# A two-part sequence model on one core: the feed-forward's tile of 43 channels projected, activated and multiplied first, and the first chunk normalised 128 tokens at a time

## The chip, the core and the metric

The kernel runs on one core of a Trainium2 chip. The core has a matrix engine (TensorE; PE in the profile, and PEld for the loading of its weights), a vector engine (VectorE, DVE), a scalar engine (ScalarE, ACT), a general engine (GpSimd, POOL) and an engine that issues transfers (SyncE, SP). Each works through its own queue of instructions in order, and semaphores order them against each other. Matrix products land in PSUM, eight banks of 128 partitions by 512 floats; all else lies in SBUF. The metric is the device time of one execution in microseconds (us), the median of several runs; lower is better.

## What is computed

The input is two sequences of 4096 tokens with 256 channels, in float32. A recurrence layer (layer norm, three projections of the token mixed with the one before it, a scan in time, a group norm, an output projection) is followed by two layers of local attention with a feed-forward network. Cut to what bears on the change:

```python
x = x + _L0_attn_ref(_layernorm(x), ...)        # the recurrence, once per sequence
h = _layernorm(x)
for l in range(2):
    h = h + local_attention(shift_token(h) @ wqkv[l], ...) @ wo[l]   # windows of 128 tokens
    n = layernorm(shift_token(h)) * ln_g[l] + ln_b[l]
    a, g = jnp.split(n @ w1[l] + b1[l], 2, axis=-1)                  # 682 channels each
    h = h + (a * gelu(g)) @ w2[l] + b2[l]
x = x + h
```

The 682 channels of the feed-forward are five full tiles of 128 partitions and a rest. With a row of ones that carries the last bias, the rest has 43 rows; without it 42.

## The kernel before

**A plan first, then the program.** The kernel does not issue its instructions as it goes. It notes every operation with its engine, its operands and an estimated cost (`note` L238, `cost` L302), and a list scheduler (`order` L376) then chooses, engine by engine, the operation that can start first and, among equals, the one with the smaller place (`o.at`: a row number given by `plan.at`, then the order of noting). Operations marked `either` go to ScalarE or VectorE, whichever is free first in the plan. `give` (L514) issues the lot from one line, so almost every instruction of the profile carries L530, and groups are told apart by the tiles that they write and read. Because the whole program comes out of one plan, moving a few operations can change the order of others far away on every engine.

**The recurrence.** `Recurrence` (L597) handles a sequence in chunks: the first sequence in 512 tokens (256 for the last two chunks), the second in 256. `normed` (L640) is its layer norm. It takes two windows of 128 tokens at a time: for each window `bn_stats` and `bn_aggr` on VectorE into one half of `r_mv`, then for both at once the power of minus one half on GpSimd (`rsqrt_of`, L556: an addition, then the power, into `r_rs`), one small product on VectorE (`r_nb`), and one scaled copy on ScalarE for each window. `transposed` (L660) turns the normalised chunk on TensorE, and `project` (L707) multiplies it with the weights `wnow` and `wold`, which are first scaled by the mixing vectors (L1429 to L1432; `scaled`, an `either` operation).

**Attention and feed-forward.** The loop over `n` (L1480) takes 128 windows of 128 tokens: two sequences, two layers, 32 windows each. Four windows make a block of 512 tokens, `k`; there are 32 blocks. The feed-forward of a block runs one to two blocks behind its attention, spread as filler between the steps of later windows (`fill`, L1352):

- `gate` (L1281) projects one tile of 128 gate channels, 512 tokens wide, into `hm`.
- `remainders` (L1289) projects the 42 gate channels and the 42 value channels of the rest together (106 rows, with a gap) and copies them apart into `ends` and `rem`. There, even windows lie on partitions 0 to 42 and odd windows on 64 to 106, so each step on the rest takes two instructions of 42 rows.
- `gelus` (L1300) is one piece on ScalarE, never interrupted by other work: five activations on `hm`, then two on `ends`.
- `value` (L1310) projects one tile of value channels and multiplies it, with its bias, into `hm` on VectorE; for the last tile (`m` = 5) it multiplies `rem` into `ends`, with no projection of its own.
- `down_ends` (L1327) starts the output sums of two windows with the 64-row product of `ends` and `w2`; `down` (L1339) adds the five products with `hm`, adds the sum to `x` and stores it.

The last block has no later windows to hide in. `last_block` (L1376) takes it in two halves of 256 tokens: transposes of the normed input `h`, five gates, the remainders, the gelus, six values in order, the two `down_ends`, the two `down`. Its value products may be issued ahead of their gelus (`plan.early`, L1312).

Of the kernel before, what the change touches and what calls it, by code (L numbers as in the profile page):

```python
# [10 lines left out]
AF = mybir.ActivationFunctionType  # L11
ALU = mybir.AluOpType
# [3 lines left out]
P = 128  # L16
# [5 lines left out]
NM = 6  # L22
# [8 lines left out]
LN_EPS = 1e-5  # L31
# [25 lines left out]


SEM = 60
OWN = {"gpsimd": 75}  # L60
LEAN = 700
SLACK = 1.06
# [118 lines left out]
class Plan:  # L181
# [35 lines left out]
    def bank(self, shape):  # L217

        return self.view(Place(T, True), 0, shape)
# [10 lines left out]
    @contextmanager  # L230
    def piece(self):

        self.open = []
        yield
        self.open = None
# [140 lines left out]
    def order(self):  # L376
# [18 lines left out]
        def ready(g):  # L395
            for e in ("scalar", "vector") if g[0].eng == "either" else (g[0].eng,):
                t, off = 0.0, 0.0
                for o in g:
                    for d in o.deps:
                        if d.eng != e:  # L400
                            t = max(t, d.end + SEM - off)
                        elif e != "tensor" and owner[d] is not g:
                            t = max(t, d.end + OWN.get(e, 30))
                    off += o.step
                waiting[e].append((t, g))

        def earliest(e, t, g):
# [4 lines left out]
            if need:  # L412
                have = sorted(b for b in banks if b is not None)
                if len(have) < need:
                    return None
                t = max(t, have[need - 1] + SEM)
            return t
# [8 lines left out]
        while todo:  # L426
# [28 lines left out]
            e = min((e for e in engines if pick[e]), key=lambda e: pick[e][0], default=None)  # L455
            assert e is not None, "no operation can start"
            t, g = pick[e]
            for o in g:
# [11 lines left out]
                step, time = o.step, o.time  # L470
                if o.eng == "either" and e == "vector":
                    n = o.outs[0].idx.size
                    time = 150 + 1.04 * n if o.name == "copy" else 155 + 0.98 * n
                    step = time - 85
# [3 lines left out]
                if e not in ("tensor", "sync"):  # L478
                    step, time = step * SLACK, time * SLACK
# [10 lines left out]
                for p in o.uses:  # L490
                    c, last = counts[p]
# [42 lines left out]
def kernel(ctx: ExitStack, tc: tile.TileContext, a: dict, out: bass.AP):  # L534
# [6 lines left out]
    tile_of, bank, piece = plan.tile, plan.bank, plan.piece  # L541
# [14 lines left out]
    def rsqrt_of(dst, var, n, eps, op):  # L556

        nc.gpsimd.tensor_scalar(dst, var, eps, None, op)
        nc.gpsimd.tensor_tensor(dst, dst, mhalf[:, :n], ALU.pow)
# [37 lines left out]
    class Recurrence:  # L597
# [42 lines left out]
        def normed(self, c):  # L640
            nw = self.len[c] // P
            x = self.chunks[c]["x"]
            for w0 in range(0, nw, 2):
                ws = range(w0, min(w0 + 2, nw))
                mv = tile_of([P, 2, 2], "r_mv", 4)
                for w in ws:
                    st = tile_of([P, 6], "r_st", 4)
                    nc.vector.bn_stats(st, x[:, w, :])
                    nc.vector.bn_aggr(mv[:, w - w0, :], st)
                rs = tile_of([P, 2], "r_rs", 4)  # L650
                rsqrt_of(rs, mv[:, :, 1], 2, LN_EPS, ALU.add)
                nb = tile_of([P, 2], "r_nb", 4)
                nc.vector.scalar_tensor_tensor(nb, mv[:, :, 0], -1.0, rs, ALU.mult, ALU.mult)
                for w in ws:
                    i = w - w0
                    nc.scalar.activation(
                        x[:, w, :], x[:, w, :], AF.Identity, bias=nb[:, i : i + 1], scale=rs[:, i : i + 1]
                    )
# [190 lines left out]
    b1 = tile_of([P, L, 2, NM], "b1")  # L849
# [34 lines left out]
    ends = tile_of([P, NW // 2, P], "ends")  # L884
# [368 lines left out]
    def transpose_h(k, w0=0, w1=NW):  # L1253
        l = blocks[k][0]
        h = hs[k]
        if w0 == 0:
            hTs[k] = tile_of([P, 2, T], "hT")
        hT = hTs[k][:, :, w0 * P : w1 * P]
        for i in range(2):
            pt = bank([P, (w1 - w0) * P])  # L1260
            for w in range(w0, w1):
                nc.tensor.transpose(
                    pt[:, (w - w0) * P : (w - w0 + 1) * P], h[:, w, i * P : (i + 1) * P], ident
                )
            g, bb = lnp[:, l, 0, i : i + 1], lnp[:, l, 1, i : i + 1]
            if i == 0:
                nc.scalar.activation(hT[:, i, :], pt, AF.Identity, bias=bb, scale=g)
            else:
                nc.vector.tensor_scalar(hT[:, i, :], pt, g, bb, ALU.mult, ALU.add)

    def hidden(k, c0, cols, ts):
        pm = bank([P, ts.stop - ts.start])
        for i in range(2):
            nc.tensor.matmul(
                pm[:cols], w1[:, i, c0 : c0 + cols], hTs[k][:, i, ts], start=(i == 0), stop=(i == 1)
            )
        return pm
# [3 lines left out]
    def gate(k, m, ts=ALL):  # L1281
        either(hm[:, m, ts], hidden(k, m * P, P, ts))

    def halves(ts):

        pairs = slice(ts.start // (2 * P), ts.stop // (2 * P))
        return [(odd, slice(64 * odd, 64 * odd + HR), pairs) for odd in range(2)]

    def remainders(k, ts=ALL):  # L1289
        pm = hidden(k, G_LAST * P, HS, ts)  # L1290
        if ts.start == 0:
            rems[k] = tile_of([P, NW // 2, P], "rem")
        for odd, rows, pairs in halves(ts):
            nc.scalar.copy(ends[rows, pairs], of_half(pm[64:HS], odd))
            either(rems[k][rows, pairs], of_half(pm[:HR], odd))

    def of_half(t, odd):
        return t.rearrange("p (w two t) -> p w two t", two=2, t=P)[:, :, odd, :]

    def gelus(k, ts=ALL):  # L1300
        l = blocks[k][0]
        with piece():
            for m in range(NM - 1):
                g = hm[:, m, ts]
                nc.scalar.activation(g, g, AF.Gelu, bias=b1[:, l, 1, m : m + 1])
            for odd, rows, pairs in halves(ts):
                g = ends[rows, pairs]
                nc.scalar.activation(g, g, AF.Gelu, bias=b1[rows, l, 1, NM - 1 : NM])

    def value(k, m, ts=ALL):  # L1310
        l = blocks[k][0]
# [15 lines left out]
    def down_ends(n):  # L1327

        k, i = (n - NW) // NW - 1, n % NW
        if not 0 <= k < NK or i > 1:  # L1330
            return
        for odd in range(2):
            rows = slice(64 * odd, 64 * odd + 64)
            pys[k, 2 * i + odd] = bank([P, D])
            nc.tensor.matmul(
                pys[k, 2 * i + odd], ends[rows, i, :], w2[rows, NM - 1, :], start=True, stop=False
            )
# [38 lines left out]
    def last_block():  # L1376

        k = NK - 1
        for w in (0, 2):
            plan.at(NN + w)  # L1380
            ts = slice(w * P, (w + 2) * P)
            transpose_h(k, w, w + 2)
            for m in range(NM - 1):
                gate(k, m, ts)
            remainders(k, ts)
            gelus(k, ts)
            for m in range(NM):
                value(k, m, ts)
            down_ends(NN + NW + w // 2)
            down(k, w)  # L1390
            down(k, w + 1)
# [88 lines left out]
    for n in range(NN + 2):  # L1480
        k, w = divmod(n, NW)
# [16 lines left out]
        first, l = ahead and (n + 1) % (NB * NW) == 0, ((n + 1) // (NB * NW)) % L  # L1498
# [140 lines left out]
```

## Time and profile before

| what | value |
|---|---|
| runs | 2951.6, 2952.49, 3802.63 us; median 2952.49 us |
| the profiled execution | 2951.72 us; its span, first to last instruction, 2949.9 us |
| mean granted TensorE clock | 0.999 |
| VectorE busy | 2236.2 us, 76% |
| ScalarE busy | 2009.6 us, 68%; 112 loads of an activation table, 1.283 us each |
| GpSimd busy | 1496.6 us, 51% |
| mean busy share of the DMA engines | 2 tenths, 66 GB/s |
| one gelu on `hm`, 128x512 | 0.709 us (155 of them) |
| one gelu on `ends`, 42x256 | 0.498 us (62 of them) |
| a power on GpSimd, 128x2 in `r_rs` | 0.773 us (32 of them) |
| a power on GpSimd, 128x1 in `rs` | 0.615 us (192 of them) |

A time in the profile counts from the start of the span. In a timeline each row has the start, the time from the first start to the last end, the engine, the line, the operation, what it writes and reads, its shape, how many equal instructions follow each other (x), and in square brackets how long the engine sat idle before it and what ended that.

### The profile page before, as it was taken

How to read it: one execution, taken by the hardware profiler on the slowest of the kernel's cores; microseconds unless marked ns; L12 is line 12 of the kernel's file. 1: busy time of each engine (PE TensorE's matmuls, PEld its weight loads, DVE VectorE, ACT ScalarE, POOL GpSimd, SP SyncE). 2: the span in 40 equal slices, each digit the busy share in tenths (PEclk: the TensorE clock that was granted, in tenths of full speed). 3: DMA queues.
4: the chain of work that ended last, by engine and by line, in shares of the span. 5: the costliest groups of instructions: out<-in, count | busy, mean ns of one | idle time of the engine just before them, and what ended most of it. 6: DMA issues, size and time to landing. Idle time of an engine off the chain costs nothing.

```text
span 2949.9 us, 49361 instructions
## 1 busy us (share of the span) xinstructions
PE 2926.3 (99%) x15468; PEld 1908.8 (65%) x15468; DVE 2236.2 (76%) x5193; ACT 2009.6 (68%) x5281; POOL 1496.6 (51%) x1831
## 2 busy tenths in 40 slices
PE   9999999999999999999999999999999999999999
PEld 4476766666666666666666666666666666666666
DVE  7889999888866987786777767777776767676764
ACT  7877788778666877776566666665666666666664
POOL 2226755555554655555655444555554555555541
PEclk9999999999999999999999999999999999999999
DMA  2323332222221211111122221121112221111110
GB/s 82 112 76 121 114 96 75 85 68 64 65 64 55 76 53 51 59 58 57 55 77 79 76 68 48 59 61 58 58 47 66 63 64 53 58 54 52 53 41 24
DMA packets 191182, 195.13 MB, mean 66 GB/s; under 512 B 34756, under 2 KB 154436, under 8 KB 190408
## 3 DMA queue, kind: packets, MB, share of 16 engines
q1 hardware_dynamic: 190920, 191.98, 21.1%
q8 instruction: 123, 2.02, 0.3%
q14 instruction: 139, 1.14, 0.1%
HBM read 85.46 MB, written 39.85 MB: 42 GB/s over the span
## 4 chain that ended last, share of the span: by engine, by line
PE 86%; ACT 6%; DVE 5%; issue 1%; POOL 0%; DMA 0%; SPq 0%; ACTq 0%; DVEq 0%
PE bank L530 86%; ACT pr L530 1%; ACT pr L526 1%; ACT L530 1%; ACT hm L530 1%; DVE hm L530 1%; DVE arena L530 1%; DVE qk L530 1%; DVE bank L530 1%; DVE sq L530 0%; ACT arena L530 0%; ACT ends L530 0%; DVE h L530 0%; DVE pB L530 0%; DVE nmx L530 0%
## 5 line engine op out<-in xcount | busy, mean ns | idle before, releaser
L530 PE MATMUL bank<-wqkv,xT 128*128 128x512 f32 x1536 | 719.2, 595 | 0.5 <-ACT xT L530 0.5
L530 PE MATMUL bank<-hT,w 128*128 128x512 f32 (+3 forms) x1452 | 650.5, 580 | 0.0
L530 POOL TENSOR_TENSOR t<-qk,tab 128x256 f32<-128x256 f32 x512 | 390.5, 781 | 412.4 <-ACT qk L530 305.3
L530 ACT ACTIVATE pr<-bank,nmx 128x129 f32<-128x129 f32 (+1 forms) x1024 | 370.5, 379 | 136.5 <-DVE nmx L530 133.2
L530 PEld LDWEIGHTS bank<-hT,w 128*128 128x128 f32 (+1 forms) x1452 | 263.9, 188 | 246.7 <-issue 235.0
L530 PEld LDWEIGHTS bank<-wqkv,xT 128*128 128x128 f32 x1536 | 267.5, 191 | 212.7 <-issue 209.3
L530 POOL TENSOR_TENSOR rn<-rn,mhalf 128x16 f32<-128x16 f32 x128 | 395.1, 3087 | 9.0
L526 ACT ACTIVATE pr<-pr,sums 128x129 f32<-128x129 f32 (+1 forms) x957 | 334.2, 420 | 30.4 <-DVE pr L530 27.1
L530 DVE COPY_PREDICATED bank<-packs,bank 128x254 f32<-128x254 int32 x496 | 186.4, 420 | 214.1 <-PE bank L530 213.7
L530 PE MATMUL bank<-w,hm 128*128 128x256 f32 x1280 | 293.8, 380 | 0.0
L530 ACT COPY qk<-bank 128x512 f32<-128x512 f32 x224 | 131.7, 588 | 194.9 <-PE bank L530 172.5
L530 PEld LDWEIGHTS bank<-w,hm 128*128 128x128 f32 x1280 | 239.6, 190 | 33.2 <-issue 2.5
L530 POOL TENSOR_TENSOR dv<-vr,vt 128x512 f32<-128x512 f32 x124 | 163.7, 1320 | 187.8 <-PE bank L530 156.5
L530 DVE TENSOR_TENSOR pB<-bank,backs 128x512 f32<-128x512 f32 x248 | 170.1, 686 | 103.7 <-PE bank L530 73.1
L530 PE MATMUL bank<-kT,qT 64*128 64x256 f32 (+1 forms) x2048 | 246.1, 380 | 1.6 <-ACT qT L530 1.6
L530 PE MATMUL bank<-wo,oT 128*128 128x256 f32 x1024 | 242.6, 380 | 0.8 <-ACT oT L530 0.8
L530 PEld LDWEIGHTS bank<-wo,oT 128*128 128x128 f32 x1024 | 193.7, 190 | 67.0 <-issue 23.1
L530 PEld LDWEIGHTS bank<-kT,qT 64*128 64x128 f32 x2048 | 190.4, 187 | 70.8 <-issue 36.1
L530 ACT COPY hm<-bank 128x512 f32<-128x512 f32 (+1 forms) x180 | 103.8, 577 | 183.5 <-PE bank L530 181.7
L530 ACT ACTIVATION_READ_ACCUMULATOR pr<-bank,nmx 128x1 f32 x1024 | 221.0, 216 | 0.0
L530 ACT COPY pT<-bank 128x512 f32<-128x512 f32 x195 | 115.6, 593 | 130.8 <-PE bank L530 94.3
L530 PE MATMUL bank<-pT,vt 128*64 128x128 f32 x2048 | 203.3, 279 | 0.0
(160 smaller groups left out, 5635.2 us busy)
## 6 DMA issues: line engine op xcount, KB each, us to landing
vr<-vt SPq DMA_DIRECT2D x124, 224.0 KB
tab<-in_c_rot_dram SPq DMA_DIRECT2D x128, 128.0 KB
kT<-kT SPq DMA_DIRECT2D x64, 256.0 KB
z<-zd SPq DMA_DIRECT2D x16, 512.0 KB
x<-in_x_dram SPq DMA_DIRECT2D x16, 512.0 KB
x1d<-x SPq DMA_DIRECT2D x16, 512.0 KB
x<-x1d SPq DMA_DIRECT2D x16, 512.0 KB
h<-x SPq DMA_DIRECT2D x128, 64.0 KB
```

What stands on the lines that cost most here:

```text
L526: self.nc.scalar.activation(dst, src, AF.Copy, scale=scale)
L530: getattr(getattr(self.nc, o.eng), name)(*args, **kw)
```

## The change

```diff
@@ the planner
+CARE = 0
-                            t = max(t, d.end + SEM - off)
+                            t = max(t, d.end + SEM + (CARE if e == "tensor" else 0) - off)
@@ Recurrence.normed
-            for w0 in range(0, nw, 2):
-                ws = range(w0, min(w0 + 2, nw))
-                mv = tile_of([P, 2, 2], "r_mv", 4)
+            step = 1 if c == 0 else 2
+            for w0 in range(0, nw, step):
+                ws = range(w0, w0 + step)
+                mv = tile_of([P, 2, 2], "r_mv", 4)[:, :step]
                 for w in ws:
                     st = tile_of([P, 6], "r_st", 4)
                     nc.vector.bn_stats(st, x[:, w, :])
                     nc.vector.bn_aggr(mv[:, w - w0, :], st)
                 rs = tile_of([P, 2], "r_rs", 4)
-                rsqrt_of(rs, mv[:, :, 1], 2, LN_EPS, ALU.add)
-                nb = tile_of([P, 2], "r_nb", 4)
+                rs = rs[:, :step]
+                rsqrt_of(rs, mv[:, :, 1], step, LN_EPS, ALU.add)
+                nb = tile_of([P, 2], "r_nb", 4)[:, :step]
@@ gelus
         with piece():
+            for odd, rows, pairs in halves(ts):
+                g = ends[rows, pairs]
+                nc.scalar.activation(g, g, AF.Gelu, bias=b1[rows, l, 1, NM - 1 : NM])
             for m in range(NM - 1):
                 g = hm[:, m, ts]
                 nc.scalar.activation(g, g, AF.Gelu, bias=b1[:, l, 1, m : m + 1])
-            for odd, rows, pairs in halves(ts):
-                g = ends[rows, pairs]
-                nc.scalar.activation(g, g, AF.Gelu, bias=b1[rows, l, 1, NM - 1 : NM])
@@ last_block
             transpose_h(k, w, w + 2)
+            remainders(k, ts)
             for m in range(NM - 1):
                 gate(k, m, ts)
-            remainders(k, ts)
             gelus(k, ts)
-            for m in range(NM):
+            for m in (NM - 1, *range(NM - 1)):
                 value(k, m, ts)
```

`CARE` is zero and alters nothing. The first chunk of each sequence (`c == 0`: four windows in the first sequence, two in the second) is normalised one window at a time. `gelus` takes the rest before the full tiles in all 32 blocks. `last_block` also projects the rest before the gates and multiplies it before the full tiles; the fillers of the other 31 blocks (`fill`) keep their order of noting.

## The prediction, made before the change was run

> **What bounds the kernel now.** I read first the busy times of the page, then the busy times by stretch of the span, since an average hides stages, then the timelines of the first 16 us and the last 30 us, and one odd spot between.
>
> ```profile
> PE 2926.3 (99%) x15468; PEld 1908.8 (65%) x15468; DVE 2236.2 (76%) x5193; ACT 2009.6 (68%) x5281; POOL 1496.6 (51%) x1831
> ```
>
> ```profile
> 0.00:20.00 20.00, 13.43 (x28) 6.18 (x29) 9.53 (x30) 9.11 (x19) 4.70 (x23) 1.00 0.47 145
> 20.00:463.00 443.00, 436.26 (x1934) 277.58 (x1933) 396.44 (x865) 353.33 (x765) 200.20 (x288) 1.00 0.29 96
> 463.00:690.00 227.00, 225.86 (x1245) 148.28 (x1244) 201.09 (x465) 175.89 (x451) 130.45 (x164) 1.00 0.25 76
> 690.00:1864.00 1174.00, 1172.58 (x6364) 769.21 (x6362) 889.86 (x2090) 797.29 (x2155) 618.81 (x737) 1.00 0.21 63
> 1864.00:2468.00 604.00, 603.93 (x3301) 393.39 (x3302) 422.63 (x997) 384.45 (x1073) 318.01 (x369) 1.00 0.20 60
> 2468.00:2900.00 432.00, 429.83 (x2378) 277.41 (x2376) 303.65 (x717) 275.27 (x785) 221.43 (x247) 1.00 0.16 48
> 2900.00:2920.00 20.00, 20.00 (x118) 16.82 (x117) 4.81 (x13) 2.93 (x8) 3.00 (x6) 1.00 0.09 28
> 2920.00:2949.90 29.90, 24.43 (x112) 19.90 (x110) 8.22 (x21) 11.37 (x29) 0.00 (x0) 0.99 0.07 22
> ```
>
> In the second view a row holds the stretch, its length, then busy us and instructions of PE, PEld, DVE, ACT and POOL. Length less PE's busy time is PE's idle time: 6.6, 6.7, 1.1, 1.4, 0.1, 2.2, 0 and 5.5 us, together 23.6 of 2949.9. A busy PE need not be a fast one, so I checked the rows of the middle: in steady state a 128x512 product follows the last after 0.43 us, a 128x256 one after 0.215, without gaps, and those intervals times the counts fill the stretches. TensorE therefore bounds everything but both ends and a few small holes. The change takes no product away, so it can win only part of those 23.6 us, and loses whatever new idle time it opens on TensorE.
>
> **The tail.** This is the first half of the last block, where TensorE's queue has nothing else left.
>
> ```profile
> 2921.37 1.28 ACT L530 ACT_TABLE_LOAD   x1
> 2922.67 2.11 ACT L530 ACTIVATE hm<-hm,b 128x256 f32<-128x256 f32 x5
> ...
> 2924.68 0.81 ACT L530 ACTIVATE ends<-ends,b 42x128 f32<-42x128 f32 x2
> ...
> 2925.52 0.71 DVE L530 SCALAR_TENSOR_TENSOR ends<-rem,b,ends 42x128 f32<-42x128 f32 x2
> 2925.90 0.68 PEld L530 LDWEIGHTS bank<-w,ends 64*128 64x128 f32 x4 [2.46 <-DVE ends L530]
> 2925.91 1.08 PE L530 MATMUL bank<-w,ends 64*128 64x256 f32 x4 [2.23 <-DVE ends L530]
> ...
> 2926.91 4.58 PE L530 MATMUL bank<-w,hm 128*128 128x256 f32 x20
> ```
>
> ScalarE does the five gelus of `hm`, then the two of `ends`; VectorE multiplies `ends` last; the product that opens the output sums needs exactly that, and TensorE sits 2.23 us idle for it.
>
> In the changed program the rest is projected first. Its four copies (0.26 each) then lie among the gates' copies, which wait for products 0.86 apart anyway; the last gate copy ends near 2920.6 (the sixth product, as the sixth result before, whose first copy started at 2920.26, plus 0.37), so the table load starts 0.7 earlier. Gelus of `ends`: 2921.95 to 2922.75. Gelus of `hm`: 2922.75 to 2924.85, as late as before (2924.78). VectorE multiplies `ends` at about 2922.4 and 2922.8. The new order on TensorE is: five products of the window before (now 2920.92 to 2923.1, and kept), first `ends` product, two transposes of `h`, second `ends` product, two transposes, then `hm`. From the rows now, the four `ends` instructions with the way to `hm` take 1.0 us (2925.91 to 2926.91), the four transposes 0.45, and a second change between 64-row and full products half of that 1.0, 0.5: `hm` starts at 2923.1 + 1.95 = 2925.0, not 2926.91. Does it then wait for VectorE? The first `hm` multiplication needs gelu one (about 2923.2), fine; the fifth ends at about 2925.65, and the fifth product of the sum comes 4 x 2 x 0.215 = 1.7 us after the first, at 2926.7: covered by 1 us. Banks: five values, one old sum and one `ends` sum are held, so the second `ends` sum and the last transposes take banks that the first `hm` multiplication (2923.7) and the add to `x` (2924.0) free; both come in time. Gain 1.9 us.
>
> In the second half the `ends` load waited 0.23 for VectorE at 2941.44; that goes: 0.2 us. After it come, as now, 4.58 us of products, the last add of 0.42 and the last store. Tail: -2.1 us; bounds 0.3 (only the wait beyond the fifth `hm` multiplication goes) and 2.5 (both waits whole).
>
> **The gelus of the other 31 blocks.** Two gelus of `ends` now stand ahead of `hm`, so each gelu of `hm` comes 1.03 us later (two in one row take 1.03). What hides it: the first value multiplication starts 1.59 to 3.5 us after its gelu is done in every one of the 31 blocks; it waits for its projection. One example: gelus from 2072.41, the first done 2073.12, its multiplication at 2075.67. So at least 0.56 us of cover stays: cost 0. Without cover it would be up to 31 x 1.03 = 32 us, since the value products hold PSUM banks until they are multiplied.
>
> **The first layer norm.** Now:
>
> ```profile
> 4.49 0.72 POOL L530 TENSOR_TENSOR r_rs<-r_rs,mhalf 128x2 f32<-128x2 f32 x1
> ...
> 9.26 2.07 PE L530 MATMUL bank<-arena 128*128 128x512 f32 x2
> 11.12 1.91 PE L530 MATMUL bank<-arena,wold 128*128 128x512 f32 x2
> ```
>
> GpSimd gets four additions and four powers for two of each. By the rows of `rs` (one element wide, 0.22 and 0.57, 0.31 from start to start) a window takes 0.88 us. The first window's statistics end at 3.55, so GpSimd starts at 3.64 and ends the fourth power at 3.64 + 4 x 0.88 = 7.16; now the second pair's (the same row again at 5.90) ends at 6.62. The first window is ready 0.7 us earlier, the last 0.5 later, but ScalarE now treats one window at the end (0.55) where it treated two (1.09): the normalised chunk is complete near 7.95 both ways. The whole chunk must be turned and copied before the first projection, so earlier windows win nothing. The added waits: ScalarE's fourth window waits for GpSimd, and behind it on ScalarE stand the scaling of `wold` and now the copy of the first turned half (0.59 on ScalarE, 0.69 on VectorE now). I take 0, bounds -0.5 and +0.5. The second sequence's first chunk adds one addition, one power and one `r_nb` of 0.18 on engines with slack: 0. No transfer is moved in either part.
>
> **What the plan shuffles.** TensorE's order is the same up to the product that ran at about 463 us, then differs up to about 640, and again in short swaps near 970 to 1060, 1170 to 1270, 1425, 2470, 2630 and 2790. ScalarE gets one table load more (113) and eight of VectorE's scalings of `pr`. There is almost nothing to win (idle from 463 to 2900: 4.8 us), and the rows cannot show new holes. I take 0; bounds -4.8, and +3.9 for each new hole, the price of the worst now, beyond 250 us:
>
> ```profile
> 252.67 3.66 PE L530 MATMUL bank<-hm,wold 128*128 128x256 f32 x8 [2.17 <-DVE hm L530]
> ```
>
> Eight such products took 1.89 at 247.44; so 2.17 idle and 1.77 of slow clock after it, 3.9 together.
>
> **Sum.** Span 2949.9 - 2.1 = 2947.8; the profiled execution 2951.72 - 2.1 = 2949.6. That execution lies 0.77 under the median of the runs, so the median becomes 2952.49 - 2.1 = 2950.4.
>
> **Rivals.**
> *Slower: a new hole in the shuffled middle.* For it: from 463 to 690 VectorE is busy 201 of 227 us, so an operation placed late there has little slack. Against: 1.1 us idle there now under a plan of the same kind. One hole like that at 252 gives 2950.4 + 3.9 = 2954.3; it decides once new idle time passes 2.1 us. Chance 0.20.
> *The clock's step moves.* Products at the start come 0.86 us apart until 13.69 and 0.43 after. I assume that this step comes after a fixed amount of work. If it doesn't, the 4.43 us from 9.26 may vanish (-2.2) or double (+2.2): 2948.2 or 2952.6. The Trainium skill (TensorE: Matmul & The Clock Gate, What's actually happening) speaks for it: the clock is released after a busy window of about 3.4 us that runs freely, not from the kernel's start. The trace agrees with a step, not yet on what sets its time; chance 0.10.
> *The tail's wait changes its name.* If a bank or the fifth multiplication holds TensorE, only 0.3 goes: 2952.2. For it: eight banks are full there. Chance 0.10.
> *More holes close.* In five places near the ends of blocks, TensorE waits some 0.5 us for `qk` (0.60 at 2663.31), where VectorE now has less to do; half of the 4.8 us gives 2948.0. Chance 0.06.
> *Far slower.* If the gelus' cover fails in the plan's new order, 30 us, still within 2%; beyond that only an execution like the 3802.63 of the three, or fifteen holes of 3.9. Chance 0.03.
> My forecast keeps the rest: 0.51, and 2949 to 2952 by itself.
>
> **Numbers.** 2950.4. Range 2946.0 to 2956.0: it takes in the clock, the tail, half of the closing holes and one new hole with 1.7 beside it, and leaves out a second hole and a full closing. Two per cent, about what a measurement of this kernel can tell from no change, is 59 us, more than twice all of TensorE's idle time: faster 0.01, same 0.96, slower 0.03.
>
> **What would show it.** Right: the wait for `ends` in the last block is gone, `hm` products start about 2 us after the products before them, `ends` gelus lead in every block with no wait of TensorE on `hm` beside them, first projection at 9.0 to 9.5 us. Wrong: PE idle over 3 us between 463 and 2900, a first projection past 10 us, or a wait on `hm` in the last block.

## The result: 7 us faster, and the profile after

The changed kernel takes 2944.99 us (median of 13 runs, 2943.61 to 2945.93). The kernel before, run beside it on the same chip, took 2952.23 us (13 runs; one of them, at 3802.63 us, was far slower than the rest and is not in the ratio). The ratio is 0.9975, with a 95% interval of 0.9968 to 0.9982: faster by about 7.2 us, far inside 2%. I had predicted 2950.4 with a range of 2946.0 to 2956.0, so the sign of the forecast was right and the time lies 1.0 us below the range. The profiled execution took 2945.01 us, its span 2943.2 us, against 2951.72 and 2949.9: 6.7 us in the span.

First the page's line of busy times, then the busy times by stretch for the changed kernel, in the columns used for the kernel before.

```profile
PE 2923.5 (99%) x15468; PEld 1909.3 (65%) x15468; DVE 2229.9 (76%) x5193; ACT 2012.7 (68%) x5285; POOL 1496.8 (51%) x1837
```

```profile
0.00:20.00 20.00, 13.39 (x28) 6.17 (x29) 9.24 (x31) 10.02 (x20) 5.84 (x27) 1.00 0.48 145
20.00:463.00 443.00, 436.25 (x1934) 277.60 (x1933) 396.43 (x866) 353.34 (x766) 200.90 (x290) 1.00 0.29 96
463.00:690.00 227.00, 225.76 (x1248) 149.06 (x1246) 204.86 (x473) 176.76 (x449) 124.39 (x163) 1.00 0.26 80
690.00:1864.00 1174.00, 1172.98 (x6372) 770.30 (x6371) 885.50 (x2086) 797.98 (x2159) 624.94 (x740) 1.00 0.21 63
1864.00:2468.00 604.00, 604.00 (x3313) 393.64 (x3314) 422.57 (x1000) 383.68 (x1073) 315.23 (x366) 1.00 0.20 59
2468.00:2900.00 432.00, 431.15 (x2376) 279.66 (x2373) 300.31 (x714) 277.14 (x790) 223.45 (x250) 1.00 0.17 48
2900.00:2920.00 20.00, 20.00 (x117) 16.43 (x115) 4.30 (x12) 7.01 (x17) 2.04 (x4) 1.00 0.09 28
2920.00:2943.20 23.20, 19.96 (x92) 16.42 (x92) 6.64 (x16) 6.80 (x19) 0.00 (x0) 0.98 0.09 29
```

TensorE's idle time from 463 to 2900 us was 4.8 us and is 3.1 now (1.24, 1.02, 0 and 0.85). From 2468 to 2900 it fell from 2.17 to 0.85. Such idle time says where, but not how much: TensorE's ends are modelled, and the waits looked at cost some 0.15 to 0.3 us more than their rows show (in the kernel before, 0.47 in the row and 0.63 by the spacing of the products at 2501 us, 0.60 and 0.76 at 2663). I therefore cut the span at two events that every kernel has, the first scores of the attention (the first row `bank<-kT,qT`) and the scores of the last window:

| stretch | before, us | after, us | change |
|---|---|---|---|
| start to first scores | 244.53 | 244.44 | -0.1 |
| first to last scores (the middle) | 2643.58 | 2639.44 | -4.1 |
| last scores to the end (the tail) | 61.83 | 59.34 | -2.5 |

So the tail gave what it should, and most of the gain came from the middle, where I had put zero. The start of the scores tells where in the middle. Up to 408 us the changed kernel is 0.1 ahead, and it is 1.4 ahead at 1086, 1.9 at 1511, still 1.9 at 2421, then 2.6 at 2505, 3.5 at 2667 and 4.2 at 2828. The last three steps, and a step of 0.5 at 1511, lie at the ends of blocks with one same hole; the 1.3 between 463 and 1086 is a net of several holes that came and went (0.53 at 489, 0.63 at 558, 0.38 at 689, 0.63 at 728 and 0.35 at 978 us before; 1.31 at 560 and 0.33 at 729 after).

The last block of the changed kernel, in the timeline:

```profile
2916.41 1.28 ACT L531 ACT_TABLE_LOAD   x1
...
2917.71 0.82 ACT L531 ACTIVATE ends<-ends,b 42x128 f32<-42x128 f32 x2
2918.14 0.77 DVE L531 SCALAR_TENSOR_TENSOR ends<-rem,b,ends 42x128 f32<-42x128 f32 x2 [2.33 <-ACT ends L531]
2918.55 2.10 ACT L531 ACTIVATE hm<-hm,b 128x256 f32<-128x256 f32 x5
...
2918.94 0.70 PE L531 MATMUL bank<-w,ends 64*128 64x256 f32 x2
...
2920.83 4.48 PE L531 MATMUL bank<-w,hm 128*128 128x256 f32 x20
```

No TensorE row of the last block carries a wait now: `ends` is multiplied while TensorE still works on the window before, and the long wait for it is gone. The start, and the worst hole beyond 250 us:

```profile
7.40 0.58 ACT L531 ACTIVATE arena<-arena,r_nb,r_rs 128x256 f32<-128x256 f32 x1
...
9.19 1.22 PE L531 MATMUL bank<-arena 128*128 128x512 f32 x1
```

```profile
252.56 3.64 PE L531 MATMUL bank<-hm,wold 128*128 128x256 f32 x8 [2.17 <-DVE hm L531]
```

The first chunk is normalised by 7.98 us and its first projection starts at 9.19 (9.26 before); the hole at 252 is as it was. Last, TensorE's waits summed by what ended them (total, times, longest):

```profile
PE bank L531 <- DVE hm L531: 2.7, 2, 2.2
PE bank L531 <- ACT qT L531: 2.1, 3, 1.2
...
PE bank L531 <- DVE qk L531: 0.2, 1, 0.2
```

The rows `DVE ends` (2.2, once) and `ACT oT` (0.8, four times) are gone, `DVE qk` fell from 1.6 in four waits to 0.2 in one, and `ACT qT` rose from 1.6 to 2.1.

### The profile page after: what moved, and what is told of

Read it like the earlier page. It is cut to its first block, busy times and chain, and to the rows that moved or that the text cites. A ratio compares the mean times of both kernels' runs of the same rounds, so it can differ in the third digit from the quotient of the medians.

```text
span 2943.2 us, 49399 instructions
## 1 busy us (share of the span) xinstructions
PE 2923.5 (99%) x15468; PEld 1909.3 (65%) x15468; DVE 2229.9 (76%) x5193; ACT 2012.7 (68%) x5285; POOL 1496.8 (51%) x1837
## 4 chain that ended last, share of the span: by engine, by line
PE 93%; DVE 3%; ACT 3%; issue 1%; DMA 0%; POOL 0%; SPq 0%; ACTq 0%; DVEq 0%
PE bank L531 93%; ACT pr L531 0%; ACT L531 0%; DVE arena L531 0%; ACT pr L527 0%; ACT hm L531 0%; ACT arena L531 0%; DVE x L531 0%; DVE qk L531 0%; DVE bank L531 0%; DVE hm L531 0%; DVE pB L531 0%; DVE h L531 0%; DVE nmx L531 0%; ACT ends L531 0%
```

## The experiments

Every kernel ran beside the kernel before, on the same chip, the changed kernels 6 to 13 times each.

| kernel | us | before beside it | ratio, 95% interval | middle | tail |
|---|---|---|---|---|---|
| before | | 2952.23 | | 2643.6 | 61.8 |
| after | 2944.99 | 2952.23 | 0.9975, 0.9968 to 0.9982 | 2639.4 | 59.3 |
| e1_tail | 2949.68 | 2952.29 | 0.9991, 0.9982 to 0.9999 | 2644.2 | 59.3 |
| e2_blocks | 2948.36 | 2952.29 | 0.9987, 0.9978 to 0.9996 | 2640.0 | 61.8 |
| e3_mask4 | 2951.94 | 2952.29 | 0.9997, 0.9988 to 1.0006 | 2643.0 | 63.3 |
| e4_gelu_only | 2950.47 | 2952.29 | 0.9993, 0.9984 to 1.0002 | 2642.6 | 61.8 |
| e5_norm | 2952.16 | 2952.67 | 0.9999, 0.9990 to 1.0008 | 2643.2 | 63.5 |
| e6_late_t | 2950.17 | 2952.67 | 0.9995, 0.9986 to 1.0003 | 2642.7 | 61.8 |
| e7_late_act | 2950.88 | 2952.67 | 0.9994, 0.9986 to 1.0003 | 2643.4 | 61.8 |
| e8_plan_only | 2946.99 | 2952.67 | 0.9982, 0.9973 to 0.9991 | 2640.8 | 59.4 |
| e9_late_act2 | 2951.60 | 2952.35 | 0.9997, 0.9988 to 1.0006 | 2642.2 | 63.5 |
| e10_pe4 | 2957.47 | 2952.35 | 1.0017, 1.0008 to 1.0026 | 2648.9 | 63.5 |
| e11_copies | 2943.54 | 2952.35 | 0.9971, 0.9959 to 0.9982 | 2638.4 | 59.4 |
| e12_copies_hm | 2942.93 | 2952.35 | 0.9969, 0.9957 to 0.9981 | 2637.4 | 59.4 |
| e13_late_all | 2950.81 | 2952.82 | 0.9995, 0.9986 to 1.0004 | 2642.1 | 63.5 |
| e14_care30 | 2945.42 | 2952.82 | 0.9975, 0.9966 to 0.9984 | 2640.2 | 59.4 |
| e15_care60 | 2953.86 | 2952.82 | 1.0005, 0.9995 to 1.0014 | 2643.8 | 59.4 |
| e16_care120 | 2947.76 | 2952.82 | 0.9983, 0.9974 to 0.9992 | 2639.3 | 59.1 |
| e17_scaled | 2951.58 | 2952.99 | 0.9996, 0.9987 to 1.0005 | 2641.5 | 63.4 |

Middle and tail are from the one profiled execution of each. Two kernels in which every engine's order in the middle is that of before, e1_tail and e5_norm, show how far a middle wanders by itself: +0.65 and -0.38. At the four block ends at 1494, 2501, 2663 and 2824 us, which the whole change shortens by 0.50, 0.69, 0.85 and 0.73 (2.8 together), they wander by -0.52, 0.08, -0.09 and 0.28, and by -0.45, 0.09, 0.39 and 0.29 (a minus is a loss; together -0.3 and 0.3). A gain at a single place is thus uncertain by some 0.4 to 0.5, and the sum of the four says more. The old tail takes 61.8 in five profiles and 63.3 to 63.5 in six: there, a slot of half clock, 3.413 us long, follows the 2.2 us wait for `ends`. The new tail takes 59.1 to 59.4 in all eight. So the tail's change is worth 2.5 us, or 4.1 where the slot would have come, which may be why the medians differ by more (7.2) than the two spans do (6.7).

Letters in the expectations stand for theories of the middle. **A**: the masks of the scores stand ahead of the scaling of `h` in VectorE's new queue. **B**: TensorE's new order, a projection ahead of two value products at four block ends. **C**: the gelus of `ends` in front by themselves. **D**, formed after the first group: VectorE's queue at those four block ends, freed by what GpSimd and ScalarE do at that time. **E**: the middle is a draw of the planner.

### Which part of the change: e1, e2, e5

Each is one part of the change alone. `e1_tail`: only `last_block`, with the lines of the change, and the gelus of its two halves. `e2_blocks`: only the gelus of the other 31 blocks. `e5_norm`: only `normed`.

```diff
@@ gelus, e1_tail (e2_blocks: k < NK - 1)
+            if k == NK - 1:
+                of_ends()
             for m in range(NM - 1):
...
+            if not (k == NK - 1):
+                of_ends()
```

> Only the last block is changed (its 43 channels first, as in the changed kernel); the other 31 blocks and the first layer norm are as before. By the terms of the prediction -2.1 us against the kernel before; by the drift that the changed kernel's trace shows behind the last full block -2.5 (hm products of the first half 1.8 nearer to the products ahead of them, those of the second half 0.6 nearer). The rival, that the tail only wins because the middle before it runs otherwise, expects under 1 us.

> Only the 31 full blocks are changed: their gelus of ends ahead of those of hm. TensorE's order then is that of the changed kernel up to the last block. If the planner's new order in the middle is the term that the prediction left out, -4.1 us (1.3 between 463 and 1045 us, 0.5 at 1494, 0.7, 0.9 and 0.7 at 2501, 2663 and 2824). If the prediction's 0 was right for it and the gain sits in the tail, 0. If the layer norm's new order has a share in the middle, between the two.

> Only the first layer norm is changed (by 128 tokens); every engine's order behind the first 20 us is that of the kernel before. By the prediction's term 0 (bounds 0.5 each way), by the changed kernel's trace -0.1. The rival, that the changed start moves the clock's step and so more, expects over 0.5 either way.

The tail alone changed its stretch by -2.47, as in the whole change. The gelus of the 31 blocks alone changed the middle by -3.6, with TensorE's order that of the whole change up to the last block. The layer norm did nothing. So 31 pairs of activations, moved by some 3 us each within ScalarE's own piece, won most of the 4 us through the planner. The next groups ask how.

### What in the new plan: e3, e4, e8, e10

Here the plan is that of one kernel, and a step behind it changes the order in a few places of one engine's queue; the queues are then merged again, with all dependences and the turns at PSUM banks kept. The lines name the operations of one queue in their order; they are not lines of the kernel, save those of the gelus.

```diff
@@ give
-        self.done = self.order()
+        self.done = self.merged(self.order(), edit)   # edit: below, for each kernel
@@ edit: e3_mask4, on before, VectorE, four windows: first two masks ahead of h
-    h scaled, mask, mask
+    mask, mask, h scaled
@@ e4_gelu_only, on before, ScalarE, all 31 pieces
+    r[i : i + 7] = g[5:] + g[:5]          # two gelus of ends, then five of hm
@@ e8_plan_only, on after, ScalarE, all 31 pieces
+    r[i : i + 7] = g[2:] + g[:2]          # the old order within the new plan
@@ e10_pe4, on before, TensorE, four windows
-    four products of two values, two of the projection
+    two of the projection, four products of two values
```

> The kernel before with one edit: at the four places ahead of the holes at 1494, 2501, 2663 and 2824 us VectorE's two first masks of the scores stand ahead of the scaling of h that waits about 1.0 us for GpSimd's rs. TensorE, ScalarE and GpSimd keep their orders and gelus keep theirs. Theory A (that in-order wait holds the softmax back by 0.7 us, and the holes are its end): the masks start 0.7 us earlier behind the scores' start and the four holes go, -2.8 us, at least -1.5. Theory B (the holes close because TensorE projects q or k ahead of two values): 0. Theory C (the gelus' order itself): 0.

> The kernel before with ScalarE's seven gelus of each of the 31 full blocks turned round (ends first) and every other instruction of every engine where it was. Theory A: the two ends products come without their wait of 0.39 us for ScalarE, so statistics, rs, h and the masks behind them come up to 0.39 earlier at the four places: about -1.6 us, no more. Theory B: 0, TensorE's order is unchanged. Theory C: the whole -2.8 or more. The prediction's cover (1.59 us and more against a shift of 1.03) expects no new wait on hm.

> The changed kernel with ScalarE's seven gelus of each of the 31 full blocks turned back (hm first, then ends); every other instruction keeps the changed kernel's order. Theory D (the gain of the middle comes from the orders that the planner gave the other engines): most of it stays, within 1 us of the changed kernel, -6 to -7 against the kernel before; VectorE's products of ends, now ahead of those of hm, wait up to 1.7 us for their gelus, which may cost 0.1 to 0.3 at the four places. Theory C (the gelus' order itself is the gain): the gain of the middle goes, about -2.6 against the kernel before is left.

> The kernel before with TensorE's order alone turned round at the four places: the projection of q or k ahead of two values, as in the changed kernel; VectorE, ScalarE and GpSimd keep their orders. Theory B (that order closes the holes): -2.8 us. Theory D: VectorE's product of the first value, which stands ahead of the layer norm's statistics and the masks, now comes 1.7 us later, so the masks start about 1.2 us later behind the scores and the four holes grow by about as much each: +3 to +6 us.

Theories A, B and C fell. The site at 2483 us, in the timelines of before, of after and of e3_mask4:

```profile
2483.25 2.00 PE L530 MATMUL bank<-kT,qT 64*128 64x256 f32 x16
...
2484.35 1.46 POOL L530 TENSOR_TENSOR t<-qk,tab 128x256 f32<-128x256 f32 x2
2484.36 0.87 DVE L530 TENSOR_SCALAR h<-h,mv,rs 128x256 f32<-128x256 f32 x1 [1.01 <-POOL rs L530]
...
2485.81 0.74 DVE L530 TENSOR_REDUCE nmx<-bank 128x2 f32<-128x258 f32 x2
...
2491.35 0.60 ACT L530 COPY qk<-bank 128x512 f32<-128x512 f32 x1
...
2493.29 1.22 DVE L530 TENSOR_REDUCE rn<-sq 128x16 f32<-128x1024 f32 x1 [1.53 <-ACT sq L530]
...
2499.73 1.45 DVE L530 TENSOR_TENSOR qk<-sq,rn 128x1024 f32<-128x1024 f32 x1
...
2501.23 0.44 PE L530 MATMUL bank<-mats,qk 128*128 128x128 f32 x2 [0.47 <-DVE qk L530]
```

```profile
2481.31 2.00 PE L531 MATMUL bank<-kT,qT 64*128 64x256 f32 x16
2481.39 0.72 POOL L531 TENSOR_TENSOR t<-qk,tab 128x256 f32<-128x256 f32 x1
...
2483.14 0.41 DVE L531 TENSOR_SCALAR h<-h,mv,rs 128x256 f32<-128x256 f32 x1
...
2483.47 0.75 DVE L531 TENSOR_REDUCE nmx<-bank 128x2 f32<-128x258 f32 x2
...
2488.66 0.60 ACT L531 COPY qk<-bank 128x512 f32<-128x512 f32 x1
...
2490.59 1.22 DVE L531 TENSOR_REDUCE rn<-sq 128x16 f32<-128x1024 f32 x1 [0.78 <-ACT sq L531]
...
2491.92 1.28 ACT L527 ACTIVATE pr<-pr,sums 128x129 f32<-128x129 f32 x4
...
2497.11 1.45 DVE L531 TENSOR_TENSOR qk<-sq,rn 128x1024 f32<-128x1024 f32 x1
...
2498.61 0.66 PE L531 MATMUL bank<-mats,qk 128*128 128x128 f32 x4
```

```profile
2485.07 0.84 DVE L576 TENSOR_SCALAR h<-h,mv,rs 128x256 f32<-128x256 f32 x1
2485.83 0.75 DVE L576 TENSOR_REDUCE nmx<-bank 128x2 f32<-128x258 f32 x2
```

Count from the first score product, S. Before, TensorE needs the rotated `qk` at S + 17.5 and gets it at S + 17.98; after, it starts at S + 17.30 without a wait. VectorE's queue leads there: the first reduction of the scores starts at S + 2.56 before and S + 2.16 after, the reduction `rn` at 10.04 and 9.28, the last product of the rotation at 16.48 and 15.80. Two things differ at its head. The scaling of `h` takes 0.87 before, beside GpSimd's two products `t`, and 0.41 after, when they are over. And ScalarE copies `qk` at S + 8.10 before and 7.35 after, with one exponential fewer ahead of it.

e3_mask4 put the masks first, as after has them, and they ran 0.74 earlier; but here, and at 2663 and 2824 us, the scaling, 0.78 to 0.84 long beside GpSimd, then stood between masks and reduction, which began where it did (2485.83 against 2485.81). At 1494 us GpSimd's first product was nearly over when the scaling began, it took 0.40, and 0.34 us were won. e4_gelu_only won 0.9 in the middle, no more; 0.6 of it at one hole (2501 us), where the new gelus happened to let `h` run in 0.42. e8_plan_only, with the old gelus in the new plan, keeps 2.7 of the 4.1. At the four block ends it wins 2.8, as much as the whole change, and 1.0 of what it loses lies at one new wait for `qk`, at 405.72 us. At the four block ends the gelus' order is thus not the cause; the plan that comes with it is. And TensorE's own new order, put into the old plan, costs:

```profile
2486.93 0.81 DVE L586 TENSOR_SCALAR h<-h,mv,rs 128x256 f32<-128x256 f32 x1 [1.01 <-POOL rs L586]
...
2491.81 1.99 PE L586 MATMUL bank<-wo,oT 128*128 128x256 f32 x8 [1.00 <-ACT oT L586]
...
2503.66 0.55 PE L586 MATMUL bank<-mats,qk 128*128 128x128 f32 x3 [0.40 <-DVE qk L586]
```

VectorE's products of the values stand ahead of the masks in its queue and now get their operands later, so the masks wait, TensorE waits 1.0 to 1.4 us for `oT` at the four places, and the whole is 5.1 us slower (interval 2.4 to 7.7 us).

### Rebuilding the gain in the old plan: e6, e7, e9, e13, e17

All are on before, at the same places.

```diff
@@ e6_late_t: GpSimd, four windows
-    t, t, dv
+    dv, t, t
@@ e7_late_act: e6, and ScalarE at two windows (2501, 2663 us)
-    exp, four scalings of pr, copy of qk
+    four scalings of pr, copy of qk, exp
@@ e9_late_act2: e6, and ScalarE at those two
-    exp, four scalings, copy of qk, exp, square, exp
+    four scalings, copy of qk, exp, square, exp, exp
@@ e13_late_all: e9, and VectorE at those two
-    reciprocal, add to pr, two scalings of pr, add to x, rn
+    add to x, rn, reciprocal, add to pr, two scalings of pr
@@ e17_scaled: e13, and the two scalings of pr go to ScalarE, ahead of its next two
+    o.eng = "scalar"
```

> The kernel before with one edit: at the four places GpSimd's two products t of the rotation stand behind dv, so that they no longer run beside VectorE's scaling of h (0.81 to 0.87 us beside them, 0.41 without them in the changed kernel). TensorE, VectorE and ScalarE keep their orders. Theory D, formed from the runs so far (the softmax starts late because h's scaling runs twice as long beside GpSimd's t; and one exponential more stands ahead of ScalarE's copy of qk): h 0.41 at all four, first reduction of the scores 0.4 earlier behind their start, the holes at 1494 and 2813 go (0.3 each) and those at 2501 and 2663 shrink from 0.6-0.8 to about 0.3: some -1.4 us. If the length of h's scaling does not matter, 0.

> As the run before, and at the two places where ScalarE copies qk (ahead of the holes at 2501 and 2663 us) that copy stands ahead of the last exponential instead of behind it, as in the changed kernel. Theory D: qk's copy another 0.34 us earlier, no hole is left at the four places, some -2.1 to -2.8 us, with TensorE's order and the gelus as before. If the exponential does not count: the same as the run before.

> The run that moved GpSimd's t at four places, and at two of them ScalarE's order as the changed kernel has it: the copy of qk ahead of the last of six exponentials, and the square behind it ahead of the next one too (in the run before this one the moved exponential came to stand ahead of the square, so rn began no sooner: 9.93 us behind the scores' start against 9.59). Theory D: rn begins near 9.3, the holes at 2501 and 2663 fall from 0.3 and 0.5 to 0.2 or less, -0.3 to -0.6 us against the run with t alone, some -2 against the kernel before. If another wait holds TensorE there, no change against the run with t alone.

> The kernel before with GpSimd's t behind dv at four places, and at two of them ScalarE's copy of qk and the square ahead of one exponential each, and VectorE's reduction rn ahead of the reciprocal and the scalings that wait for the exponential so moved. TensorE and the gelus as before. Theory D: rn begins near 9.3 us behind the scores' start (10.04 before, 9.92 in the run without VectorE's part), TensorE's waits for qk at 2501 and 2663 are gone, and the trace is some 2 us ahead of the kernel before by 2830 us. If TensorE's order is needed for the second half of those holes: 0.3 of each stays.

> The run before last but three (t late at four places; qk's copy, square and rn ahead at two) and, at those two places, the two scalings of pr that VectorE did behind rn (0.48 us) done by ScalarE ahead of its next two. Theory D in full (VectorE's queue between the scores and the rotation is the path; the changed kernel takes 0.4 of h's scaling and 0.4 of these scalings off it): the rotation's last product starts near 15.9 us behind the scores' start (16.34 without, 15.80 in the changed kernel), TensorE's waits of 0.35 and 0.21 for qk go, and by 2830 us the trace is 2.0 to 2.6 us ahead of the kernel before, with TensorE's order and the gelus' as before. If something else holds the rotation: 16.3, and the waits stay.

In e6_late_t, GpSimd's products no longer touch the scaling of `h`:

```profile
2484.07 0.41 DVE L577 TENSOR_SCALAR h<-h,mv,rs 128x256 f32<-128x256 f32 x1 [1.01 <-POOL rs L577]
...
2485.06 0.75 DVE L577 TENSOR_REDUCE nmx<-bank 128x2 f32<-128x258 f32 x2
...
2488.16 1.42 POOL L577 TENSOR_TENSOR t<-qk,tab 128x256 f32<-128x256 f32 x2
```

It takes 0.41 at all four places. At three, the first reduction starts at S + 2.1 and the hole shrinks from 0.63 to 0.28 (2501 us), from 0.76 to 0.53 (2663), and to nothing (2813), these sizes counted from the spacing of the products; at the first (1494), the scaling came late and the hole stayed. At the four places together it wins 1.2 us of the 2.8. (The hole at 2663 us also fell, to 0.21 in its row from 0.60, in e5_norm, whose order there is that of before: the firm evidence is where the reduction starts, not the size of one hole.)

The other half resisted twice. e7_late_act had the copy of `qk` at S + 7.34, but the exponential that it passed landed ahead of the square, and `rn` began at S + 9.93. e9_late_act2 gave ScalarE its order of after, square included, and `rn` still began at S + 9.93: VectorE's queue held a reciprocal, an addition and two scalings of `pr` ahead of it, which now waited for the moved exponential. With `rn` ahead of these (e13_late_all) it began at S + 9.24, and then the same four stood ahead of the rest of the rotation, whose last product came at S + 16.34. Only when the two scalings of `pr` were also handed to ScalarE, as the new plan has it, did the path come out:

```profile
2483.15 0.41 DVE L617 TENSOR_SCALAR h<-h,mv,rs 128x256 f32<-128x256 f32 x1 [1.01 <-POOL rs L617]
...
2491.28 1.22 DVE L617 TENSOR_REDUCE rn<-sq 128x16 f32<-128x1024 f32 x1 [0.86 <-ACT sq L617]
...
2492.67 1.28 ACT L613 ACTIVATE pr<-pr,sums 128x129 f32<-128x129 f32 x4
...
2497.85 1.41 DVE L617 TENSOR_TENSOR qk<-sq,rn 128x1024 f32<-128x1024 f32 x1
...
2499.32 0.87 PE L617 MATMUL bank<-mats,qk 128*128 128x128 f32 x6
```

S is 2482.04 here: `rn` at S + 9.24, the last product at S + 15.81 (after: 15.80), TensorE at S + 17.28 without a wait (after: 17.30), with TensorE's order and the gelus untouched. Against before it wins 0.71 at 2501, 0.68 at 2663, 0.56 at 2824 and 0.25 at 1494 us, 2.2 together, where the whole change wins 0.69, 0.85, 0.73 and 0.50, or 2.8. Theory D stands at the two places that were rebuilt whole, 2501 and 2663; at the other two only GpSimd's products were moved, and one more scaling of `pr` that the new plan hands to ScalarE at each was left. The medians cannot confirm it: 0.9996 is 1.4 us faster, and the interval, 0.9987 to 1.0005, takes in both nothing and the trace's 2.1.

### Is the rest a draw: e14, e15, e16

```diff
@@ on after
-CARE = 0
+CARE = 30      # e15_care60: 60, e16_care120: 120
```

This only makes the planner believe that TensorE sees results so much later; what is computed stays, and the order comes out otherwise.

> The changed kernel with the planner told to expect results 30 ns later on TensorE (CARE 30 in place of 0): the same work, other orders from 55 us on. Theory E (the middle is a draw: any small change of the plan moves some holes and the sum by a few us either way, the first layer norm and the tail stay): 2940 to 2952, and the holes sit elsewhere. Theory F (the gelus' order makes the plan better for a lasting reason): within 1 us of the changed kernel's 2945.0, without holes for qk at the ends of blocks.

> As the run before with 60 ns. Theory E: 2938 to 2952, another set of holes. Theory F: within 1 us of 2945.0.

> As the run before with 120 ns, more than the plan needs: results come to TensorE early in truth, so waits get rarer and products are put off for nothing where the plan now sees idle time. Theory E: 2938 to 2955. Theory F: within 1 us of 2945.0.

Three other plans of the same change took 2945.42, 2953.86 and 2947.76: a spread of 8.4 us, wider than the change's whole effect. Most of the losses lie ahead of 1350 us (in e15_care60 a wait of 3.6 us at 178 and the slow clock after it, and 1.55 at 517); between 1350 and 2300 us e14_care30 and e15_care60 lose another 1.3 and 2.1 against the changed kernel. From the scores at 2301 us to those of the last window, though, the three lie within 0.6 us of the changed kernel, where the kernel before takes 2.3 more, and no wait of TensorE for `qk` is left there. So E holds up to that point, and the three late block ends are no draw: every such plan that I ran closes them.

### A better version: e11, e12

```diff
@@ e11_copies: on after, ScalarE, two windows (560 and 1243 us)
-    activation and table load for the recurrence, copies of kT and qT
+    copies of kT and qT, activation and table load
@@ e12_copies_hm: e11, and VectorE in the first window (252 us)
-    cosine, cosine, reciprocal, sum, reciprocal, hm, hm
+    cosine, hm, hm, reciprocal, cosine, reciprocal, sum
```

> The changed kernel with one edit on ScalarE: ahead of the two largest holes that it has left in the middle (560.15 and 1242.89 us) the copies of kT and qT stand ahead of an activation of the recurrence and the table load of 1.28 that it brings. If those holes are that in-order wait, TensorE's waits of 1.24 and 0.62 go: -1.9 us against the changed kernel, about 2943. If the recurrence's chain, now 0.6 to 1.1 later, makes TensorE wait elsewhere, part comes back: between 2943 and 2945.

> The run before, and ahead of the hole at 252.5 us (2.17, the largest of both kernels) VectorE's two products of hm stand ahead of the rotation's second cosine product and sum, so that TensorE's next products could start about 1.4 us sooner. If that hole costs what the prediction put on it (2.2 of wait and 1.8 of slow clock): -1 to -4 us against the run before. In three profiled runs no slot of slow clock followed the hole, and by 278 us TensorE was no further ahead for it, since it waited elsewhere; by that reading the gain is small, 0 to -1.

The holes for `qT` at 560 and 1243 us, which the new plan had made wider, closed: 1.30 and 0.64 won, 0.8 of it given back at 565 and 596 us, and 2943.54 in all. e12_copies_hm takes away the 2.17 us wait at 252 us, but TensorE, 2.6 us ahead of the changed kernel at 259 us (0.3 of it from the start), then waits elsewhere:

```profile
265.34 1.99 PE L592 MATMUL bank<-wo,oT 128*128 128x256 f32 x8 [1.26 <-ACT oT L592]
```

Net 0.6. At 2942.93 it is the best of all, 0.9969 of before (interval 0.9957 to 0.9981); that it beats the changed kernel by 2 us is a comparison of medians, each against before.

## Why the prediction was wrong by a little

**The step that failed** is the one headed "What the plan shuffles". It said "There is almost nothing to win (idle from 463 to 2900: 4.8 us), and the rows cannot show new holes. I take 0", and it measured -4.1, close to the -4.8 that it gave as its bound. Two things went wrong in it. The idle column understates what holes cost, so more could be won than it shows. And I took the reshuffle as a draw around zero, though the rows of before showed the same wait for `qk` at one kind of place, and eight scalings of `pr` had left VectorE's queue on balance; by the two traces it is six at the four block ends (over the whole span other operations took their place: 5193 instructions before and after). Together these give a direction, not a draw. The rival "More holes close" named the place, the wait and the engine; I gave it half of the idle time, -2.4, and 0.06. (It counted five such waits of some 0.5; TensorE has four of `qk`, from 0.18 to 0.60, and two of them lie at these block ends.) By the scores' starts 2.8 of the 4.1 lie at the four block ends, and e17_scaled rebuilds 2.2 of them. The cause of the other 1.3, ahead of 1086 us, stays open: the three other plans make a draw likely, but I have not followed its holes one by one. The range reached only to half of the closing, and so missed by 1.0. Of the 5.4 us between 2950.4 and 2944.99, the middle makes 4.1, the tail 0.4 and the start 0.1; the remaining 0.8 lies between the profiled executions and the medians.

**The tail** was right in mechanism: -2.1 predicted, -2.5 measured. Its first half gave 1.85 (the `hm` products at 2920.83 against 2926.91, less the 4.23 by which the last scores came earlier), where 1.9 was predicted. The second half gave 0.6, where I counted only the 0.23 of idle time: the way from its first `ends` product to its first `hm` product took 1.14 us before and 0.63 after, so the wait cost twice what its row showed. That is the same error of reading as in the middle. What I had not priced is the slot of half clock behind the old wait, 1.6 us when it falls.

**The gelus' cover** held: no wait of TensorE on `hm` appears beside them in the middle, and in e4_gelu_only, where they alone move, nothing is lost.

**The layer norm** gave the zero predicted: chunk complete at 7.98 (7.95 predicted), first projection at 9.19 (9.0 to 9.5; 9.56 in e5_norm, which waited for DMAs at 4.38 and 5.97 us), and 0.9999 for e5_norm.

**The rival of a new hole** came about (0.63 at 558 us grew to 1.31 at 560) and was outweighed; its price, 3.9, was too high. The row that I priced it by was 2.17 of wait and 1.77 of slow clock. The slow clock costs nothing there, as shown below, and e12_copies_hm, without the wait, won only 0.6. **The clock's step** did not decide: 13.56 us after against 13.71 before. My assumption that it follows a fixed amount of work is wrong all the same. **The tail's wait** did not change its name. **A sign of being wrong** was badly chosen: TensorE idle over 3 us between 463 and 2900 us. It was 4.8 already before, and 3.1 after, so the sign is met although the idle time fell. Nor is 2% about what a measurement can tell here: the interval above is 0.07% to either side.

## What to carry to other kernels

When an edit feeds a list scheduler, compare all engines' queues at the places where the bounding engine already waits, and follow the path to that wait on the other engines: here what left those queues gave 2.2 us rebuilt in the old plan and 2.8 in the new one, where the moved gelus themselves cost nothing. A plan changed elsewhere by chance (here a spread of 8.9 us over four plans) is best tried in several versions. An idle figure of TensorE is not a price: the waits for `qk` cost 0.15 to 0.3 us more than their rows show, while the wait of 2.17 at 252 us gave 0.6 when it was removed. Measure a hole by how far later products shift. Putting one queue of a better plan into an older one can lose (5.1 us here), since the queues fit each other.

## What the hardware showed that I had not expected

**VectorE slows beside GpSimd.** The scaling of `h` (128x256 float32, SBUF to SBUF) takes 0.41 us alone and, at the four block ends of the kernel before, 0.80 to 0.87 beside GpSimd products of the same size (0.72 each), as the rows above show. The Trainium skill (SBUF — State Buffer, SBUF: two separate sides) says that VectorE, in some of its modes or with two inputs in SBUF, and GpSimd share a pair of ports under an exclusive lock, held for the whole instruction of whichever starts first. e6_late_t agrees that the two contend: move the GpSimd products, and the scaling is back at 0.41. The 19 traces agree on the whole instruction too. In all 803 cases where a GpSimd product of 128x256 or 128x512 was running when the scaling began, with more than 0.28 us left, the scaling ended 0.15 us (0.145 to 0.156) behind that product's end. At 2484.36 us in before the product had begun 0.01 us earlier, and the scaling took 0.87; beside the longer product `dv` it mostly takes 1.4.

**The clock's step is not the kernel's.** Full clock is first granted between 11.23 and 14.16 us in 19 profiles, all with a first projection at 9.07 to 9.56, and the full and half stretches between are multiples of 3.413 us. The Trainium skill (TensorE: Matmul & The Clock Gate, What's actually happening) has a window of 3413 ns that runs freely; the traces agree. The start moves with it by up to 1.5 us: in the 17 kernels other than e15_care60 and e16_care120, whose plans lose time ahead of the first scores, these start between 243.31 us (step at 11.23) and 244.76 (step at 14.16).

**The same hole, another clock.** Behind the same 2.17 us wait at 252 us, the half clock lasts 3.413 us in before and after, 6.827 in e7_late_act, and does not come in e4_gelu_only. In the busy times of that stretch the granted clock is the column after the engines (0.50 in before, 1.00 in e4_gelu_only):

```profile
252.70:255.60 2.90, 2.90 (x7) 2.18 (x8) 2.90 (x3) 2.35 (x5) 2.90 (x3) 0.50 0.24 90
```

```profile
252.70:255.60 2.90, 2.90 (x19) 2.62 (x18) 2.90 (x3) 2.20 (x4) 2.90 (x3) 1.00 0.31 117
```

In these 2.9 us TensorE does 19 products where it did 7; but e4_gelu_only is 1.22 us further on in its work, and shorter products are among the 19. On the same work, the eight `hm` products behind the wait, the time to the next product is 3.49 us in before and 2.26 here. By 278 us TensorE is no further ahead than at 244 all the same (1.22 and 1.23 us): it waits for `qk` at 256.79, `oT` at 265.12 and `pr` at 269.54 instead. Here the slow clock, ahead of waits that take its place, cost nothing.
